# Interleaving expert steps with layer 3 in a four-layer attention chain, and moving one bias addition

## The chip, the cores and the metric

The kernel runs on one core of one Trainium2 chip. The time is the device time of one launch in microseconds (us), and the median of several runs is compared. The engines of the core are PE (TensorE, matrix multiplication, with PEld as its weight loads), DVE (VectorE), ACT (ScalarE), POOL (GpSimd) and SP (SyncE, which only issues transfers here). Each engine works through its own list of instructions in order.

## The reference

64 sequences of 128 tokens and 128 features pass through four layers in turn. Each sequence has a context of 77 rows. Cut to what matters here:

```
x = L0(ctx, x)        # layer norms, a small cross attention, a self attention
x = L1(x, ctx, ctx)   # linear attention with elu, residual, layer norm
# layer 2: self attention and cross attention of 16 heads of width 8, then 8 experts
x = x + mha(ln(x), ln(x));   x = x + mha(ln(x), ln(ctx))
h = ln(x);  top 2 of 8 experts by h @ router;  gates = softmax of the two
x = x + sum_k gate_k * (gelu(h @ w1[e_k] + b1[e_k]) @ w2[e_k] + b2[e_k])
# layer 3: causal self attention, cross attention, feed-forward, each with a layer norm after it
x = ln(x + sa(x) @ Wo + bo);  x = ln(x + ca(x, ctx) @ Wo + bo)
x = ln(x + relu(x @ W1 + b1) @ W2 + b2)
```

## The kernel before, in words

The 64 sequences are cut into 16 groups of 4 (`NB`); two groups make a set for the experts (`SG`), so there are 8 sets. The work of a group is written as Python generators. Each `yield` ends one step, and the order in which steps are emitted is written out by hand in the loop at lines 898 to 912. The framework derives the semaphores and may move instructions of neighbouring steps past each other on an engine, but the loop sets which steps stand side by side.

- `front` (L467) does layers 0 and 1 of a group in 7 steps.
- `middle` (L581) does layer 2 up to the router: two calls of `mha` of 8 steps each, then two steps for the router and the gates, and a last one that stores the group, so 19 in all. `firsts` (L874) runs `middle` of one group beside `front` of the next, so in steady state a group takes 19 rounds, and the first half of the kernel (layers 0 to 2) ends with round 299.
- `dispatch` (L666) works out for a set which token goes to which row of a DRAM buffer, in 2 steps, and scatters the tokens with 16 indirect transfers on POOL (L739), two to a step.
- `experts` (L755) works through the 23 tiles of 128 rows (`NT`) of a set, one tile to a step. It reads three tiles at once (L761), loads each tile's two expert matrices on SP (L774, L777, 256 KB each), and does a small bias product (L782), the first matrices (L787), one Gelu on ACT (L792) and the second matrices (L794). The result goes back to DRAM (L801). There are 184 such steps.
- `second_half` (L805) is layer 3 of a group. It gathers the experts' answers with 8 indirect transfers on POOL (L817), then calls `mha` twice and does the feed-forward, 18 steps. At most two groups are in it at once, in lanes 1 and 0; lane 0 is opened only when the first half is over. The dictionary `thirds` holds those that are open.

In every round of the loop, the first half gets one step (`ahead` is true while it lasts), then the dispatch, then perhaps the experts (L903), then each open layer-3 group.

`mha` (L336) has three parts. Its first step makes QT, KX and the values, and adds the residual and the output bias `bo` on POOL (L371) into `dst`; with `resid` None, as in layer 3's cross attention, it doesn't. Six steps then work on the four sequences in a pipeline: scores and softmax of sequence i (L387 to L399, in a PSUM tile `banks` of which there is one), the transposes of sequence i-1 (L409, L410), and the weighted sum and division of sequence i-2 (L417 to L432). The last step multiplies by the output matrix and adds to `dst` (L460). So the sum with `bo` is needed only at L460, seven steps after the first.

Of the kernel before, what the change touches and what calls it, by code (L numbers as in the profile page):

```python
# [11 lines left out]
ALU = mybir.AluOpType  # L12
# [9 lines left out]
NB = 4  # L22
# [30 lines left out]
def bc(ap, axis, n):  # L53

    ap = ap.unsqueeze(axis)
    shape = list(ap.shape)
    shape[axis] = n
    return ap.to_broadcast(shape)
# [11 lines left out]
def tile_xattn_chain(  # L70
# [21 lines left out]
    V, S, G, T = nc.vector, nc.scalar, nc.gpsimd, nc.tensor  # L92
# [13 lines left out]
    def bank():  # L106
        return ps1.tile([P, 512], F32, tag="bank", name="bank")
# [43 lines left out]
    row = {n: row_sb[:, i, :] for i, n in enumerate(ROWS)}  # L151
# [100 lines left out]
    n = x.shape[0] // NB  # L252
# [53 lines left out]
    def copy_t(src, p=P, **where):  # L306
        pool, tag = where.get("pool", work), where.get("tag", "tT")
        dst = pool.tile([P, NB * p], F32, tag=tag, name=tag, bufs=where.get("bufs"))
        S.copy(dst, transposed(src, p))
        return dst  # L310
# [25 lines left out]
    def mha(n, lane, qT, kT, nk, resid, dst, is_causal=False):  # L336
# [26 lines left out]
        for k, at in enumerate((0, 48)):  # L363
# [3 lines left out]
                bc(row[f"{n}_bv"][:nk], 1, NB).rearrange("k b (h i d) -> k b h i d", i=2, d=DH)[:, :, :, k],  # L367
                ALU.add,
            )
        if resid is not None:  # L370
            G.tensor_tensor(dst, resid, bc(row[f"{n}_bo"], 1, NB), ALU.add)  # L371
        yield
        O = work.tile([P, NB, P], F32, tag="O", name="O")

        def softmax(b):

            sc = banks()
            if is_causal:
                for g in range(4):
                    T.matmul(  # L380
                        sc[:, g, :], lhsT=ident16, rhs=causal16.rearrange("p j k -> p (j k)"),
                        start=True, stop=False,
                    )

            for g in range(4):
                part = slice(32 * g, 32 * g + 32)
                T.matmul(  # L387
                    sc[:, g, : NJ * nk].rearrange("q (j k) -> q j k", j=NJ),
                    lhsT=QT[part, b, :], rhs=KX[part, :, b, :nk],
                    start=not is_causal, stop=True,  # L390
                )
            halves = []
            for half in range(2):
                scores = sc[:, 2 * half : 2 * half + 2, : NJ * nk].rearrange("q i (j k) -> q i j k", j=NJ)
                m = small.tile([P, 2, NJ], F32, tag="m", name="m")
                recent["max"] = V.tensor_reduce(m, scores, AX.X, ALU.max)  # L396
                pr = attn.tile([P, 2, NJ, nk], F32, tag="pr", name="pr", bufs=4)
                V.tensor_tensor(pr, scores, bc(m, 3, nk), ALU.subtract)  # L398
                S.activation(pr, pr, AF.Exp, scale=DH**-0.5)  # L399
                halves.append(pr)  # L400
            return halves

        def turned(pr):

            pT = attn.tile([P, 2, NJ, P], F32, tag="pT", name="pT")
            for i in range(2):
                pt = bank()
                for j in range(NJ):
                    T.transpose(pt[:nk, j * P : (j + 1) * P], pr[:, i, j, :], ident)  # L409
                S.copy(pT[:nk, i].rearrange("k j q -> k (j q)"), pt[:nk])  # L410
            return pT

        def weighted(b, half, pT, po):

            for k in range(2):
                for g in range(4):
                    T.matmul(  # L417
                        po[32 * g : 32 * g + 32, half * P : half * P + P],
                        lhsT=vp[:nk, b, 4 * half + g, 32 * k : 32 * k + 32], rhs=pT[:nk, g // 2, g % 2 * 2 + k, :],
                        start=k == 0, stop=k == 1,  # L420
                    )

        def divided(b, po):
            oT = work.tile([P, 2, P], F32, tag="oT", name="oT")
            S.copy(oT.rearrange("p r q -> p (r q)"), po)
            on = bank()
            for r in range(2):
                T.transpose(on[:, r * P : (r + 1) * P], oT[:, r, :], ident)  # L428
            heads = on[:, 0 : 2 * P].rearrange("q (h c) -> q h c", c=16)
            rs = small.tile([P, NH], F32, tag="rs16", name="rs16")  # L430
            V.reciprocal(rs, heads[:, :, DH])  # L431
            V.tensor_tensor(  # L432
                O[:, b, :].rearrange("q (h d) -> q h d", d=DH), heads[:, :, 0:DH], bc(rs, 2, DH), ALU.mult
            )

        probs, turns = {}, {}
        for i in range(NB + 2):
            if i < NB:
                probs[i] = softmax(i)
            if i >= 2:  # L440
                po = pso.tile([P, 2 * P], F32, tag="po", name="po")
            if 0 <= i - 1 < NB:
                halves = probs.pop(i - 1)
                turns[i - 1, 0] = turned(halves[0])
            if i >= 2:
                weighted(i - 2, 0, turns.pop((i - 2, 0)), po)
            if 0 <= i - 1 < NB:
                turns[i - 1, 1] = turned(halves[1])
            if i >= 2:
                weighted(i - 2, 1, turns.pop((i - 2, 1)), po)  # L450
                divided(i - 2, po)
            yield
        OT = copy_t(O)
        ps = bank()
# [350 lines left out]
    def second_half(st, lane):  # L805
        t = st["t"]
        i = t // SG
        x4 = stream("x4")
        nc.sync.dma_start(out=x4.rearrange("q b d -> q (b d)"), in_=later_x[t])
        CT = work.tile([P, NB * SK], F32, tag="CTr", name="CTr", bufs=2)  # L810
        nc.sync.dma_start(out=CT, in_=later_c[t])
        se = st["set"]
        for b in range(NB):
            c = t % SG * NB + b
            for k in range(2):
                ans = work.tile([P, P], F32, tag="ans", name="ans", bufs=3)
                G.indirect_dma_start(  # L817
                    out=ans, out_offset=None, in_=answered[i],
                    in_offset=bass.IndirectOffsetOnAxis(ap=se["rows_i"][:, k, c : c + 1], axis=0),
                )  # L820
                V.scalar_tensor_tensor(
                    x4[:, b, :], ans, se["gates"][:, k, c : c + 1], x4[:, b, :], ALU.mult, ALU.add
                )
        yield


        xT = copy_t(x4)
        xs = stream("xs")
        yield from mha("3s", lane, xT, xT, P, x4, xs, is_causal=True)
        xh = normalize(xs)  # L830
        xT = affine_t(xh, "g1", "be1")
        xs = stream("xs")
        affine(xs, xh, "g1", "be1")
        yield from mha("3c", lane, xT, CT, SK, None, xs)
        xh = normalize(xs)
        xT = affine_t(xh, "g2", "be2")
        xs = stream("xs")
        affine(xs, xh, "g2", "be2")
        h1 = hidden(xT, ff_w1_sb, ff_b1_sb, AF.Relu)
        V.tensor_tensor(xs, xs, back(h1, ff_w2_sb), ALU.add)  # L840
        y = work.tile([P, NB, P], F32, tag="y", name="y", bufs=2)
        affine(y, normalize(xs), "g3", "be3", G)
        nc.sync.dma_start(out=out[t * NB : (t + 1) * NB].rearrange("b q d -> q b d"), in_=y)
        yield
# [29 lines left out]
    def firsts():  # L874


        yield from begun(0)
        yield from beside(beside(middle(states[0], 0), second_group()), begun_late(2, 19))
        done.extend(range(SG))
        for t in range(2, n):  # L880
            yield from beside(middle(states[t], 0), begun(t + 1) if t + 1 < n else iter(()))
            done.append(t)

    def sends():
        for i in range(n_sets):
            while (i + 1) * SG - 1 not in done:
                yield
            yield from dispatch(i)
            sent_sets.append(i)

    def seconds():
        for i in range(n_sets):
            while i not in sent_sets:
                yield
            yield from experts(i)
            answered_sets.append(i)

    first, send, second, thirds, t = firsts(), sends(), seconds(), {}, 0
    step = 0
    while t < n or thirds:  # L900
        ahead = next(first, "end") != "end"
        next(send, None)
        if step % 2 == 0 or not ahead:  # L903
            next(second, None)

        for lane in (1, 0):
            if lane not in thirds and t < n and t // SG in answered_sets and (lane or not ahead):
                thirds[lane] = second_half(states[t], lane)
                t += 1
            if lane in thirds and next(thirds[lane], "end") == "end":  # L910
                del thirds[lane]
        step += 1
# [74 lines left out]
```

## Time and profile before

| what | value |
|---|---|
| median of 3 runs | 3913.91 us (3906.8 to 3919.5) |
| the profiled execution's own time | 3934.11 us |
| its span, first to last instruction | 3932.3 us |
| PE busy | 3022.6 us, 77% |
| PE weight loads busy | 2063.3 us, 52% |
| DVE busy | 2153.0 us, 55% |
| ACT busy | 1977.9 us, 50% |
| POOL busy | 519.4 us, 13% |
| DMA moved | 180.81 MB, mean 46 GB/s |
| granted TensorE clock, mean | 0.832 of full |

"Busy" is time in which an engine executes; the shares are means over stages that differ. A "granted clock" below 1 means that matrix instructions ran slower for part of the time. Each view names an instruction by its line in the kernel and by the tiles that it writes and reads (out<-in). The windows view gives, for a stretch of the span, its length and then for each engine the busy time and, in brackets, the number of instructions, then the granted clock, the share of time the DMA engines were busy, and the GB/s.

### The profile page before, as it was taken

To read this page: it belongs to the slowest core of one execution; us is meant where nothing else is said; L and a number is where in the kernel's file an instruction comes from. 1 tells how busy PE (TensorE), PEld (TensorE's weight loads), DVE (VectorE), ACT (ScalarE), POOL (GpSimd) and SP (SyncE) were. 2 spreads that over 40 slices of the span, in tenths; PEclk is the share of its full clock that TensorE was granted. 3 is DMA by queue.
4 is the path that set the end of the run, shared out by engine and by line. 5 is a ranking of instruction groups with operands and counts; after the bars stand their busy time and mean duration, and the time that the engine had idled before them with its cause. 6 is when DMAs were issued, how large, how long until landed. Compare 5 with 4: busy or idle time off the path is not lost. (4 is left out here: it accounts for less than half of the span.)

```text
span 3932.3 us, 59072 instructions
## 1 busy us (share of the span) xinstructions
PE 3022.6 (77%) x22735; PEld 2063.3 (52%) x22797; DVE 2153.0 (55%) x5292; ACT 1977.9 (50%) x2994; POOL 519.4 (13%) x506
## 2 busy tenths in 40 slices
PE   3675677778778778787778877878878888878777
PEld 2454455545455555555455555656545555545544
DVE  5656454456465564555556645566445635445354
ACT  2443353545365554555454635656446556536344
POOL 1002101110211101101211012010210121020110
PEclk9776776878788787978788977989778989989988
DMA  5001111110111111111111011111111132222100
GB/s 178 2 10 35 45 37 55 48 43 30 47 37 43 46 37 33 43 38 52 39 32 53 28 55 39 41 37 36 37 46 40 43 104 65 63 83 64 62 8 6
DMA packets 168257, 180.81 MB, mean 46 GB/s; under 512 B 15708, under 2 KB 111784, under 8 KB 167848
## 3 DMA queue, kind: packets, MB, share of 16 engines
q1 hardware_dynamic: 157936, 157.03, 12.8%
q0 software_dynamic: 8192, 16.79, 1.4%
q8 instruction: 181, 2.97, 0.3%
q10 hardware_dynamic: 1848, 3.19, 0.2%
q14 instruction: 100, 0.82, 0.1%
HBM read 133.54 MB, written 43.42 MB: 45 GB/s over the span
## 5 line engine op out<-in xcount | busy, mean ns | idle before, releaser
L410 ACT COPY pT<-bank 77x512 f32<-77x512 f32 (+1 forms) x1024 | 565.8, 584 | 454.1 <-PE bank L409 410.5
L409 PE MATMUL bank<-ident,pr 128*128 128x128 f32 (+1 forms) x4096 | 661.5, 304 | 146.6 <-ACT pr L399 89.1
L396 DVE TENSOR_REDUCE m<-banks 128x8 f32<-128x1024 f32 (+1 forms) x512 | 514.6, 1005 | 432.3 <-PE banks L387 431.7
L409 PEld LDWEIGHTS bank<-ident,pr 128*128 128x128 f32 (+1 forms) x4096 | 506.7, 158 | 358.8 <-ACT pr L399 134.4
L398 DVE TENSOR_TENSOR pr<-banks,m 128x1024 f32<-128x1024 f32 (+1 forms) x512 | 513.7, 1003 | 26.7 <-PE bank L409 3.1
L399 ACT ACTIVATE pr<-pr 128x1024 f32<-128x1024 f32 (+1 forms) x512 | 451.5, 888 | 122.9 <-DVE pr L398 120.7
L387 PE MATMUL banks<-KX,QT 32*128 32x512 f32 (+1 forms) x2048 | 450.7, 659 | 51.7 <-DVE pr L398 39.6
L280 POOL TENSOR_TENSOR rs<-ve,mhalf 128x4 f32<-128x4 f32 (+1 forms) x160 | 164.4, 1027 | 2379.7 <-DVE ve L278 2379.3
L417 PE MATMUL po<-pT,vpad 77*32 77x128 f32 (+1 forms) x8192 | 435.3, 290 | 17.9 <-issue 8.2
L417 PEld LDWEIGHTS po<-pT,vpad 77*32 77x32 f32 (+1 forms) x8192 | 246.1, 112 | 145.8 <-issue 109.0
L794 PE MATMUL bank<-we,he 128*128 128x128 f32 x1472 | 246.1, 318 | 63.8 <-ACT he L792 60.7
L794 PEld LDWEIGHTS bank<-we,he 128*128 128x128 f32 x1472 | 209.9, 220 | 131.5 <-ACT he L792 103.7
L787 PEld LDWEIGHTS bank<-xT,we 128*128 128x128 f32 x1472 | 229.8, 227 | 60.7 <-ACT xT L769 32.6
L787 PE MATMUL bank<-xT,we 128*128 128x128 f32 x1472 | 241.9, 316 | 18.5 <-ACT xT L769 14.4
L296 PE MATMUL bank<-ident,xh 128*128 128x128 f32 (+1 forms) x448 | 97.0, 340 | 196.5 <-DVE xh L283 179.7
L792 ACT ACTIVATE he<-bank 128x512 f32<-128x512 f32 x184 | 109.9, 597 | 236.0 <-PE bank L787 227.8
L431 DVE RECIPROCAL rs<-bank 128x16 f32<-128x16 f32 x256 | 64.8, 253 | 290.3 <-PE bank L428 286.1
L387 PEld LDWEIGHTS banks<-KX,QT 32*128 32x128 f32 x2048 | 135.9, 213 | 144.2 <-issue 92.4
L739 POOL DMA_INDIRECT sent<-xm,rows_i x128 | 126.0, 984 | 525.7 <-DVE m L396 168.7
L296 PEld LDWEIGHTS bank<-ident,xh 128*128 128x128 f32 (+1 forms) x448 | 64.9, 167 | 223.5 <-issue 161.3
L792 ACT ACT_TABLE_LOAD x124 | 159.1, 1283 | 37.5 <-PE bank L787 35.5
L303 ACT ACTIVATE tT<-bank,col_sb 128x512 f32<-128x512 f32 x80 | 62.3, 778 | 182.6 <-PE bank L296 172.8
(242 smaller groups left out, 4055.3 us busy)
## 6 DMA issues: line engine op xcount, KB each, us to landing
we<-in_moe_w_dram SPq DMA_DIRECT2D x368, 256.0 KB
sent<-zero SPq DMA_DIRECT2D x56, 192.0 KB
xe<-sent SPq DMA_DIRECT2D x56, 192.0 KB
answered<-ye SPq DMA_DIRECT2D x56, 192.0 KB
X<-in_x_dram SPq DMA_DIRECT2D x16, 256.0 KB
later_x<-x3b SPq DMA_DIRECT2D x16, 256.0 KB
x<-later_x SPq DMA_DIRECT2D x16, 256.0 KB
out_dram<-y SPq DMA_DIRECT2D x16, 256.0 KB
```

The lines of the kernel that those rows point to most:

```text
L280: G.tensor_tensor(rs[:p], ve[:p], mhalf[:p], ALU.pow)
L296: T.transpose(ps[:, b * p : (b + 1) * p], src[:, b, :], ident[:p, :p])
L387: T.matmul(sc[:, g, : NJ * nk].rearrange("q (j k) -> q j k", j=NJ), lhsT=QT[part, b, :], rhs=KX[part, :, b, :nk], start=not is_causal, sto ...
L396: recent["max"] = V.tensor_reduce(m, scores, AX.X, ALU.max)
L398: V.tensor_tensor(pr, scores, bc(m, 3, nk), ALU.subtract)
L399: S.activation(pr, pr, AF.Exp, scale=DH**-0.5)
L409: T.transpose(pt[:nk, j * P : (j + 1) * P], pr[:, i, j, :], ident)
L410: S.copy(pT[:nk, i].rearrange("k j q -> k (j q)"), pt[:nk])
L417: T.matmul(po[32 * g : 32 * g + 32, half * P : half * P + P], lhsT=vp[:nk, b, 4 * half + g, 32 * k : 32 * k + 32], rhs=pT[:nk, g // 2, g % ...
L787: T.matmul(ps[:, c * P : (c + 1) * P], lhsT=we[:, 0, c, :], rhs=xT[:, a * P : (a + 1) * P], start=False, stop=c == NC - 1,)
L792: S.activation(he.rearrange("p c q -> p (c q)"), ps, AF.Gelu)
L794: T.matmul(eo[:, a * P : (a + 1) * P], lhsT=he[:, c, :], rhs=we[:, 1, c, :], start=c == 0, stop=c == NC - 1)
```

## The change

Two edits. In the loop, the experts were stepped in each even round, and in every round once the first half was over; now they are stepped in each even round, and in every round in which no layer-3 group is open at that point. In `mha`, the addition of residual and `bo` on POOL moves from the first step to the third of the six pipeline steps.

```diff
@@ mha, first step
-        if resid is not None:
-            G.tensor_tensor(dst, resid, bc(row[f"{n}_bo"], 1, NB), ALU.add)
         yield
         O = work.tile([P, NB, P], F32, tag="O", name="O")
@@ mha, for i in range(NB + 2)
                 weighted(i - 2, 1, turns.pop((i - 2, 1)), po)
                 divided(i - 2, po)
+            if i == 2 and resid is not None:
+                G.tensor_tensor(dst, resid, bc(row[f"{n}_bo"], 1, NB), ALU.add)
             yield
@@ the loop
-        if step % 2 == 0 or not ahead:
+
+        if step % 2 == 0 or not thirds:
             next(second, None)
```

## Prediction

> **What bounds the kernel now.** I read the engine table first, then the windows by stage and by group, the waits, and the timeline of the tail. The page says that no single engine is full:
>
> ```profile
> PE 3022.6 (77%) x22735; PEld 2063.3 (52%) x22797; DVE 2153.0 (55%) x5292; ACT 1977.9 (50%) x2994; POOL 519.4 (13%) x506
> ```
>
> So the time is made of chains that overlap imperfectly: a round costs what its streams (layers 0 and 1, layer 2, experts, layer 3) cannot hide behind each other. I cut the span by stage: after the first half (to 3163), the tail up to the end of set 6's experts (3474), the pair of groups 12 and 13 with set 7's experts (3723), the last pair alone.
>
> ```profile
> 810.00:3163.00 2353.00, 1883.30 (x14194) 1273.76 (x14233) 1347.75 (x3265) 1255.93 (x1890) 316.49 (x302) 0.83 0.13 40
> 3163.00:3474.00 311.00, 260.88 (x2114) 182.61 (x2121) 146.69 (x333) 169.84 (x256) 47.42 (x46) 0.94 0.26 80
> 3474.00:3723.00 249.00, 198.14 (x1563) 137.95 (x1571) 115.56 (x230) 129.17 (x194) 26.58 (x26) 0.89 0.22 69
> 3723.00:3933.00 210.00, 143.94 (x1157) 90.11 (x1164) 109.17 (x223) 86.81 (x143) 26.47 (x26) 0.84 0.03 9
> ```
>
> The reader is to see that the last stage, two layer-3 groups without experts, takes 210 us with PE busy only 144, so the stage before it carries set 7's 23 expert steps for only 39 us more. To price a layer-3 group beside the first half, I cut the first half by group (the Gelus at L792 and the exponentials at L399 appear in the order of the steps, so counting them dates each round):
>
> ```profile
> 341.00:493.00 152.00, 104.88 (x740) 76.31 (x741) 80.96 (x219) 63.94 (x99) 26.80 (x26) 0.71 0.15 47
> 493.00:659.00 166.00, 125.50 (x807) 86.69 (x806) 78.93 (x210) 77.88 (x112) 10.84 (x10) 0.74 0.14 46
> 838.00:1068.00 230.00, 182.03 (x1377) 121.93 (x1381) 132.05 (x322) 116.73 (x181) 21.36 (x20) 0.83 0.12 37
> ```
>
> Each is 19 rounds: with 5 expert steps and a dispatch; with 10 expert steps; with 10 expert steps and one whole layer-3 group. In the tail, experts alone come every 3.0 us:
>
> ```profile
> 3719.37 0.60 ACT L792 ACTIVATE he<-bank 128x512 f32<-128x512 f32 x1 [1.96 <-PE bank L787]
> 3722.38 0.60 ACT L792 ACTIVATE he<-bank 128x512 f32<-128x512 f32 x1 [2.42 <-PE bank L787]
> ```
>
> **What the Trainium skill says.** "Perfetto Trace Analysis", Identifying the Most-Contended Engine: matmul busy share is no measure of how near PE is to its limit, the weight-load share is a better one. The trace agrees that PE isn't full: weight loads are at 52%. "TensorE: Matmul & The Clock Gate", Part 1: PE falls to half clock after idle windows and comes back with sustained work. The granted clock was 0.71 to 0.74 in the two windows without layer 3 above and 0.83 in the one with it, which fits. "ScalarE: Activation LUTs", What ACT_TABLE_LOAD costs: 1283 ns plus a drain per change of function set; the L792 and L399 loads here are 1283 ns each, 124 and 108 of them. "Perfetto Trace Analysis", Tensor Engine Instruction: GpSimd's queue is strictly first in, first out, so an addition placed there delays what is behind it.
>
> **The change, part by part.** No instruction is added or removed; both edits move work. I ran the loop by hand with the yields of each generator.
>
> | | before | after |
> |---|---|---|
> | rounds | 375 | 374 |
> | layer-3 groups begun at rounds | 90, 109, 136 ... 293 | 67, 86, 116 ... 282 |
> | groups done inside the first half (to round 299) | 9 and 0.55 of the tenth | 11 |
> | expert steps up to round 299 | 128 | 147 |
> | expert steps beside first half and layer 3 | 84 | 94 |
> | beside first half only | 44 | 53 |
> | beside layer 3 only | 48 | 19 |
> | alone | 8 | 18 |
>
> *Layer 3 moved into the first half: +81 us.* A line through the twelve windows of one group each, from 493 us on, gives 165.6 us, plus 6 with a dispatch, plus 55.9 (standard error 7) for each whole layer-3 group beside it. 1.45 groups more cost 1.45 x 55.9 = 81. Bounds: 47 to 73 (the latter from a fit over all step types).
>
> *Nineteen more expert steps in the first half: +65 us.* The added price of a step there isn't seen alone. Its PE instructions take 0.38 + 1.05 + 1.16 + 0.2 = 2.8 us in the timeline. The window 341 to 493 had 4.5 fewer steps than the line's mean and took 152 against 165.6 + 6.2 = 171.8, 4.3 each; the front halves of two windows (0 and 4 steps, both with dispatch; 81.9 and 91.6 us) say 2.4. I take 3.4: 19 x 3.4 = 65. Bounds 1.4 (below) to 4.3; not below zero, since the PE work is real and PE is the busiest engine there.
>
> *The stretch from round 300 to the end of set 6: -168 us.* Before, it took 311 us: half of group 9, the pair 10 and 11, 33 expert steps. After, it holds group 11 alone with 9 expert steps, then 5 steps alone. A lone layer-3 group isn't in the profile. I build it from the last pair, whose exponentials date it: 34 us from the last Gelu to the first exponential, eight softmaxes of 7.7 (to 3820), 24 to the cross attention (3844), eight of 4.8 (to 3882), 50 to the end. Alone: 15 (8 gathers at 1.25 us instead of 16, and no wait for answers), 4 x 7.7 = 31, 20, 4 x 4.8 = 19, and 30 until the experts stand alone, so 115. Nine expert steps beside it at 1.4 make 128, and 5 x 3.0 = 15 follow: 143. 311 - 143 = 168. Upper bound of the lone group: only the second lane's softmaxes fall away from the pair, 210 - 31 - 19 = 160.
>
> *The pair 12 and 13: +7 us.* It hid 18 expert steps; the stage from 3474 to the 19th (3711) took 237, against about 200 for the last pair without its final store, so 2.1 each. With a step every second round only 10 lie beside it and 13 stand alone: 8 x (3.0 - 2.1) = 7. Bounds 0 to 16 (if the eight were hidden for 1.0). The last pair, 210 us, is unchanged.
>
> *The bias addition: -8 us.* 48 additions of 1.27 us, done by POOL, 61 us at most. DVE waited for POOL's `rs` (L280) for 163 us in 141 waits, 1.16 each, where `rs` itself takes 1.02; queueing is thus at most 20 us in all. The addition also stands among the 16 gathers that begin a pair, where it delays the next by one place. On the other side it can meet another stream's `rs` in its new round, at the same price. I take -8; bounds -20 to +10. The cover is the four steps left before L460.
>
> *The start of a layer-3 group: +5 us.* In rounds without layer 3 the experts' end is noticed one round later and not two, so the first gather follows the set's last expert step by one round in the first half. The tail shows 5 us from the last Gelu to the first gather (3722.4 to 3727.3). POOL waits in that time, and `rs` of the first half is queued behind it, with DVE's normalization waiting for that. Six times 0 to 5 us: 0 to 30. The reads at L761 now also follow the last scatter by one round in two sets, behind which SP's weight loads wait; I put that in the same sum.
>
> Sum: 81 + 65 - 168 + 7 - 8 + 5 = -18. The profiled execution's own time goes from 3934 to 3916. The median of the runs stands at 3913.91 / 3934.11 = 0.9949 of it: 3916 x 0.9949 = **3896 us**. A measurement here can tell about 0.3% (12 us) from no change.
>
> **The rivals.** *The experts are hidden in the first half.* For it: PE is busy only 75% in the windows without layer 3, at a clock of 0.74, and more matrix work can raise the clock. Against: the two estimates of 2.4 and 4.3. At 1.4 a step and a lone group of 115 us the sum is -18 - 38 - 13 = -69: 3845 us on the median's scale. *The lone group is a chain that nothing fills (slower).* Place: rounds 300 to 317, where lane 1 is empty, because set 6's answers are not ready. Price: each us of that group over 128 goes to the end. From 146 us on the gain is gone; at its bound of 160 the sum is +14 and 3928 us. For it: a single `banks` tile and one stream, so PE, DVE and ACT take turns, and PE cools. Against: half of group 9 with 10 expert steps and a dispatch took some 75 us in the trace. *The schedule only trades places.* The experts' and layer 3's work is the same, and 375 rounds become 374: within 12 us, 3914 us.
>
> **How the numbers follow.** The forecast 0.40, experts hidden 0.20, lone chain 0.27, traded places 0.13. Faster by over 0.3% is the first two, 0.60; same 0.13; slower 0.27. The forecast's own range is 3870 to 3905. The range of 8 in 10 reaches down to the hidden experts and up past the lone chain with expert steps at 4.3 (+17): 3842 to 3945. Both signs have weight; the likeliest case is faster.
>
> **What would show it.** In the changed kernel's trace: group 11 alone from about 3310 us on, for 115 to 130 us until the experts stand alone (more than 146 refutes the sum); 13 Gelus at 3.0 us before the last pair, where there were 5; the first half's end about 146 us later than 3163; the window of one group with a layer-3 group beside it still near 222 us; POOL's addition never followed by a longer wait of DVE for `rs` than 1.2 us in the mean. The prediction is wrong if a window without layer 3 and with an expert step in every round grows by more than 4.3 us a step, or if the first half stalls at the new gathers.

## The result, and the profile after

The changed kernel takes 3971.53 us (median of 4 runs, 3963.38 to 3980.23), the kernel before in the same runs 3912.03 us. The ratio is 1.0145, with a 95% interval of 1.0121 to 1.0170: slower by some 57 to 60 us, where 18 us less were forecast.

The profiled execution of the kernel after took 3963.38 us, with a span of 3961.6. That is 8 us under its median, while the profiled execution of before was 22 us above its own. So the two traces show a difference of 29 us, and not the whole 59. The rest can't be looked up in them, and the experiments below are therefore read by their medians and ratios first.

The engine line of the page after says, like that of before, that no engine is full:

```profile
PE 3052.0 (77%) x22797; PEld 2071.5 (52%) x22797; DVE 2147.2 (54%) x5292; ACT 1963.6 (50%) x2978; POOL 517.1 (13%) x506
```

PE's busy time seems to have grown by 29 us, but 62 of before's matmul records are missing (22735 of 22797; all are of the mask matmul, L380, which keeps PE busy for about 0.35 us), some 22 us. It is not a finding.

The windows by stage say more. I cut both traces at events that both have: the first expert Gelu, the first exponential of group 15's cross attention (the last group to pass through the first half), the last Gelu of set 6 and the last of set 7. First the kernel before:

```profile
433.00:3072.00 2639.00, 2083.18 (x15492) 1419.62 (x15526) 1479.08 (x3657) 1378.56 (x2069) 352.63 (x337) 0.82 0.13 42
3072.00:3474.00 402.00, 338.98 (x2701) 233.01 (x2713) 198.14 (x455) 222.61 (x334) 57.95 (x56) 0.93 0.24 73
3474.00:3723.00 249.00, 198.14 (x1563) 137.95 (x1571) 115.56 (x230) 129.17 (x194) 26.58 (x26) 0.89 0.22 69
3723.00:3933.00 210.00, 143.94 (x1157) 90.11 (x1164) 109.17 (x223) 86.81 (x143) 26.47 (x26) 0.84 0.03 9
```

And the kernel after:

```profile
431.00:3258.00 2827.00, 2265.11 (x16773) 1533.86 (x16777) 1562.97 (x3843) 1479.91 (x2215) 375.99 (x361) 0.83 0.14 44
3258.00:3500.00 242.00, 189.02 (x1469) 131.47 (x1467) 111.04 (x270) 116.43 (x181) 32.62 (x32) 0.85 0.20 61
3500.00:3749.00 249.00, 195.25 (x1571) 134.27 (x1571) 113.22 (x230) 119.76 (x186) 26.41 (x26) 0.91 0.22 67
3749.00:3962.00 213.00, 146.77 (x1164) 90.34 (x1164) 109.34 (x223) 87.22 (x144) 26.34 (x26) 0.83 0.03 9
```

The first numbers are the stretch and its length, then PE's busy time. The first half grew from 2639 to 2827, by 188 us. The three stages behind it fell from 861 to 704, by 157, nearly all of it in the first of them (402 to 242). The prediction had +146 and -161 there, with the cut at round 300, ten rounds behind the exponential used here. Round 300 has a Gelu in both kernels, at 3167.52 us in before and 3359.04 in after (the timeline of ACT, one line of each):

```profile
3167.52 0.60 ACT L792 ACTIVATE he<-bank 128x512 f32<-128x512 f32 x1 [0.34 <-PE bank L787]
3359.04 0.60 ACT L792 ACTIVATE he<-bank 128x512 f32<-128x512 f32 x1 [1.31 <-PE bank L787]
```

With that cut it is +193 up to there and -162 behind. So the loss is in the first half. PE's busy time rose by 182 us there (170 with the 34 missing records counted), and its idle time did not fall (556 to 562): the work that came in filled no gap.

The tail did what was forecast. Set 6's last five Gelus now stand alone, at the same pace as before (the timeline of ACT):

```profile
3488.56 0.60 ACT L792 ACTIVATE he<-bank 128x512 f32<-128x512 f32 x1 [1.31 <-PE bank L787]
3491.57 0.60 ACT L792 ACTIVATE he<-bank 128x512 f32<-128x512 f32 x1 [2.42 <-PE bank L787]
...
3499.74 0.60 ACT L792 ACTIVATE he<-bank 128x512 f32<-128x512 f32 x1 [2.42 <-PE bank L787]
```

The first half by group, again dated by counting Gelus and exponentials. These are the three windows of the kernel after that answer to 341 to 493, 493 to 659 and the one behind it. They hold 10, 13 and 5 expert steps, and none, 0.41 and one whole layer-3 group:

```profile
340.00:509.50 169.50, 122.11 (x833) 89.52 (x834) 82.53 (x222) 71.29 (x108) 26.77 (x26) 0.73 0.20 63
509.50:706.70 197.20, 147.45 (x1120) 100.71 (x1119) 110.77 (x266) 107.19 (x153) 27.58 (x26) 0.83 0.15 46
706.70:918.40 211.70, 176.38 (x1290) 118.11 (x1290) 128.17 (x310) 111.79 (x173) 33.81 (x33) 0.82 0.13 39
```

In the first of them only expert steps were added: five more for 17.5 us, 3.5 each. That is what the prediction had for one step (3.4).

A window with a layer-3 group beside the first half was to stay near 222 us. Two later ones, with a dispatch and most of a group (0.74 and 0.90), came out at 250 and 248. Of all these windows they lie furthest above the forecast; the one behind the second took 200 with a whole group. One window is therefore no measure of a group:

```profile
1583.80:1833.90 250.10, 209.15 (x1249) 138.09 (x1250) 114.26 (x284) 119.26 (x169) 38.28 (x38) 0.73 0.14 44
2054.40:2302.30 247.90, 195.05 (x1386) 129.42 (x1387) 136.44 (x341) 126.61 (x188) 47.10 (x45) 0.82 0.15 47
```

Of the waits, these rows of the kernel before (line, tile, what it waited for; us in total, times, longest us)

```profile
DVE xh L283 <- POOL rs L280: 146.8, 125, 7.0
DVE x L821 <- DMA ans<-answered,rows_i: 73.6, 66, 5.2
POOL ans L817 <- DMA answered<-ye: 43.5, 2, 31.6
```

became these after:

```profile
POOL ans L817 <- DMA answered<-ye: 158.8, 6, 53.9
DVE xh L283 <- POOL rs L280: 138.5, 124, 7.7
DVE x L821 <- DMA ans<-answered,rows_i: 97.2, 73, 7.1
```

POOL now waits six times, not twice, for the last answers of a set to land before it can gather them. It looks like the cause, and one of my theories was built on it. The experiments took it apart.

### The profile page after: what moved, and what is told of

It is laid out like the page before. It is cut to its first block, busy times and chain, and to the rows that moved or that the text cites. A ratio compares the mean times of both kernels' runs of the same rounds, so it can differ in the third digit from the quotient of the medians.

```text
span 3961.6 us, 59113 instructions
## 1 busy us (share of the span) xinstructions
PE 3052.0 (77%) x22797; PEld 2071.5 (52%) x22797; DVE 2147.2 (54%) x5292; ACT 1963.6 (50%) x2978; POOL 517.1 (13%) x506
## 5 line engine op out<-in xcount | busy, mean ns | idle before, releaser
L407 PE MATMUL bank<-ident,pr 128*128 128x128 f32 (+1 forms) x4096 | 670.2, 307 | 153.2 <-ACT pr L397 87.4
L394 DVE TENSOR_REDUCE m<-banks 128x8 f32<-128x616 f32 (+1 forms) x512 | 515.0, 1006 | 438.5 <-PE banks L385 428.4
L396 DVE TENSOR_TENSOR pr<-banks,m 128x616 f32<-128x616 f32 (+1 forms) x512 | 514.4, 1005 | 25.6 <-PE bank L407 2.8
L397 ACT ACTIVATE pr<-pr 128x616 f32<-128x616 f32 (+1 forms) x512 | 451.9, 888 | 149.2 <-DVE pr L396 137.3
L385 PE MATMUL banks<-KX,QT 32*128 32x512 f32 (+1 forms) x2048 | 477.9, 648 | 54.7 <-DVE pr L396 33.6
L415 PE MATMUL po<-pT,vpad 128*32 128x128 f32 (+1 forms) x8192 | 432.9, 289 | 15.2 <-ACT pT L408 13.5
L415 PEld LDWEIGHTS po<-pT,vpad 128*32 128x32 f32 (+1 forms) x8192 | 242.7, 112 | 147.0 <-issue 104.8
L385 PEld LDWEIGHTS banks<-KX,QT 32*128 32x128 f32 x2048 | 144.5, 210 | 152.9 <-issue 95.4
L817 POOL DMA_INDIRECT ans<-answered,rows_i x128 | 124.1, 970 | 265.6 <-DMA answered<-ye 158.8
```

Source lines behind the costliest of these rows:

```text
L385: T.matmul(sc[:, g, : NJ * nk].rearrange("q (j k) -> q j k", j=NJ), lhsT=QT[part, b, :], rhs=KX[part, :, b, :nk], start=not is_causal, sto ...
L415: T.matmul(po[32 * g : 32 * g + 32, half * P : half * P + P], lhsT=vp[:nk, b, 4 * half + g, 32 * k : 32 * k + 32], rhs=pT[:nk, g // 2, g % ...
```

## The experiments

Each ratio is to the kernel before, run on the same chip; the interval is 95%. Theory A began as: the loop edit costs it, because layer-3 groups begin in rounds that no expert step fills. From e5 on it was narrower: layer 3 now starts right behind the last expert step of its set, POOL waits there for the answers, and this costs more than 5 us a set. Its rivals were B, that the thinned expert steps in the tail lose time, and C, that the bias addition does.

| run | edit | median us | ratio |
|---|---|---|---|
| after | both edits | 3971.5 | 1.0145 (1.0121 to 1.0170) |
| e1 | loop edit alone | 3960.3 | 1.0114 (1.0090 to 1.0137) |
| e2 | bias edit alone | 3895.9 | 0.9939 (0.9916 to 0.9962) |
| e3 | after, tail dense again | 3947.4 | 1.0073 (1.0051 to 1.0095) |
| e5 | after, layer 3 one round later | 3917.5 | 1.0010 (0.9990 to 1.0030) |
| e6 | e5 and e3 | 3878.3 | 0.9900 (0.9873 to 0.9927) |
| e7 | after, layer 3 two rounds later | 3919.1 | 1.0022 (1.0008 to 1.0037) |
| e8 | bias edit, layer 3 one round later | 4034.4 | 1.0311 (1.0286 to 1.0335) |
| e9 | after, rows sent gathered | 3916.1 | 1.0012 (0.9991 to 1.0034) |
| e10 | before, rows sent gathered | 3860.0 | 0.9862 (0.9832 to 0.9892) |
| e11 | e6, bias addition back | 3884.3 | 0.9905 (0.9873 to 0.9938) |
| e12 | bias edit, layer 3 two rounds later | 3994.1 | 1.0199 (1.0168 to 1.0230) |
| e13 | before, expert steps moved alone | 3842.6 | 0.9834 (0.9808 to 0.9860) |
| e14 | e13, rows sent gathered | 3841.9 | 0.9839 (0.9814 to 0.9864) |
| e15 | before, layer 3 moved alone, rows sent gathered | 3921.5 | 1.0031 (1.0014 to 1.0047) |
| e16 | e1, rows sent gathered | 3906.2 | 0.9994 (0.9980 to 1.0009) |

**One edit at a time (e1, e2).**

```diff
@@ e1: the kernel before, with
-        if step % 2 == 0 or not ahead:
+        if step % 2 == 0 or not thirds:
@@ e2: the kernel before, with the addition moved from the first step to `if i == 2 and resid is not None`
```

> The loop edit alone; the bias addition stays in the first step of mha. Theory A (the loop edit costs it: layer-3 groups begin in rounds that have no expert step to fill them, and the first half grows by more than the tail gives back): slower than before by 45 to 70 us, like the whole change. Theory C (the bias addition, later in POOL's queue, does it): within 12 us of before.

> The bias edit alone; the loop as before. Theory A: within 12 us of before, with 8 us of gain as the prediction had it. Theory C: slower than before by 40 to 60 us.

The loop edit alone costs 1.14%, 45 us. The bias edit alone gains 0.61%, 24 us, more than forecast. They don't add up: 45 - 24 is 21, and the kernel with both is slower by 57. Why they meet so badly was not looked into. C is out as the cause of the whole, since the loop edit alone costs 45.

**The thinned tail (e3).**

```diff
-        if step % 2 == 0 or not thirds:
+        if step % 2 == 0 or not thirds or not ahead:
```

> The whole change, but experts stepped in every round again once the first half is over. The first half is that of the changed kernel. Theory A: still slower than before by 40 to 65 us, since the tail after the first half took as long as predicted. Theory B (thinning the experts in the tail costs it): back to within 15 us of before.

With a step in every round of the tail again, 0.72% (28 us) come back. B has a part in what is left on the table, but the kernel stays slower than before.

**Layer 3 starts later (e5, e6, e7).** A set counts as answered one round (e7: two rounds) after the loop has noticed it:

```diff
-    step = 0
+    step, noticed = 0, {}
...
+        for i in answered_sets:
+            noticed.setdefault(i, step)
         for lane in (1, 0):
-            if lane not in thirds and t < n and t // SG in answered_sets and (lane or not ahead):
+            if lane not in thirds and t < n and t // SG in answered_sets and step > noticed[t // SG] and (lane or not ahead):
```

> The whole change, but a layer-3 group begins one round later after its set's last expert step, as far behind it as before the change. Theory A in its narrow form (POOL waits in the first gather for the answers to land, and the normalizations of the first half wait behind it): gets back 20 to 40 us of the 60. If only the missing expert steps beside the start matter, or the experts' price: within 12 us of the changed kernel.

> The whole change, with a layer-3 group begun one round later after its set's last expert step, and experts in every round again after the first half. If the start (54 us) and the thinned tail (24 us) are separate costs, both are gone: about 3893 us, 0.5% faster than before, within 12 us of the bias edit alone (3896), which would say that dense experts in the first half bring nothing by themselves. If they overlap: 3905 to 3920.

> The whole change, with the start two rounds later. Theory A (from the last Gelu of a set to the first exponential of its layer-3 group is a chain of some 36 us that cannot be shortened, so each further round that stands inside it is nearly free): 10 to 40 us faster than with one round later, down to 3880 to 3905. If one round was all that the answers need to land (5 us): within 12 us of one round later (3917).

One round takes back 53 us of the 57, more than A's 20 to 40, and a second round gives nothing further. With the dense tail as well (e6) the kernel is faster than before by 1.0%. The stages of e5 and e6:

```profile
429.00:3208.00 2779.00, 2220.65 (x16668) 1507.22 (x16713) 1561.82 (x3838) 1468.41 (x2208) 377.12 (x362) 0.84 0.14 45
3208.00:3446.00 238.00, 187.72 (x1519) 131.45 (x1525) 108.89 (x275) 119.00 (x186) 31.52 (x31) 0.89 0.19 61
```

```profile
430.00:3203.00 2773.00, 2214.28 (x16670) 1499.99 (x16716) 1563.06 (x3838) 1469.32 (x2210) 376.16 (x362) 0.84 0.14 45
3203.00:3395.00 192.00, 159.63 (x1340) 111.16 (x1347) 97.24 (x235) 110.23 (x169) 28.23 (x28) 0.95 0.24 75
```

The gain of e5 is in the first half: 2827 to 2779.

**The same delay without the loop edit (e8, e12).** The kernel of e2 with e5's and e7's start.

> The bias edit alone (loop as before), with the start one round later than there. Theory A: there the chain already has one more round in it than in the changed kernel, so the gain is smaller, 0 to 25 us under 3896. If only the wait for the answers mattered: no gain, within 12 us of 3896.

> The bias edit alone, with the start two rounds later; one round later cost 138 us, which no theory here had. If layer 3 is worse the later it stands: 4040 us or more. If it is the place of layer 3's steps against the first half's that decides (each has its layer norm and its queries, keys and values in one step): different again, 3880 to 3960.

Every theory missed these. One round later costs 3.7% against e2 (146 us), two rounds 2.6%. The first half of e8 is 2735 us against e2's 2624 (windows cut at the same events; e2 first, then e8):

```profile
429.00:3053.00 2624.00, 2069.84 (x15496) 1408.90 (x15534) 1481.99 (x3659) 1379.19 (x2070) 350.61 (x336) 0.83 0.13 42
```

```profile
428.00:3163.00 2735.00, 2106.64 (x15479) 1427.57 (x15520) 1484.11 (x3656) 1386.24 (x2073) 350.05 (x337) 0.81 0.13 40
```

The same instructions, the same number of expert steps, every layer-3 group shifted by one round: +111 us. So "a later start is cheaper" is no rule. Where layer 3's steps stand against the first half's can weigh more than the 81 us that I charged for layer 3.

**No wait for the answers (e9, e10).** Layer 3 gathers the rows that were sent to the experts instead of their answers, so nothing in it waits for an expert step, while its groups still begin in the same rounds. The output is therefore another one.

```diff
-                    out=ans, out_offset=None, in_=answered[i],
+                    out=ans, out_offset=None, in_=sent[i],
```

> The whole change, but layer 3 gathers the rows that were sent to the experts in place of the experts' answers, so the result is another one; the gathers themselves stay, and nothing in layer 3 waits for the set's last expert step any more. Theory A: most of the 54 us comes back, 3905 to 3940, since the chain can begin before the last Gelu. If the cost is only that the eight gathers and their sums on DVE stand in a round without expert steps: within 15 us of the changed kernel's 3972.

> The kernel before, but layer 3 gathers the rows that were sent to the experts in place of their answers, so the result is another one: the control for the same edit on the changed kernel, which gained 56 us. Theory A (before the change, one more round stands between a set's last expert step and its first gather, and the chain of some 40 us is covered by four rounds): 0 to 20 us faster than before. If the edit gains by something else than the start (lighter gathers, an easier end): about 50 us faster here too.

In the changed kernel this gives 52 us, the same as e5. But e10, the control, gives 54 us in the kernel before as well. The wait is dear, and it was there already. With it gone from both, the changed kernel is still slower by 59 us (e9 against e10), as with it (57). So A falls as the cause of the loss. In its place I put a last theory, D: one of the two streams that the loop edit moves, the expert steps or layer 3, costs more at its new rounds than the sum charged.

**The bias addition in the repaired kernel (e11).** e6 with the addition back in the first step.

> The loop edit with both repairs (start one round later, experts in every round after the first half), and the bias addition back in the first step of mha: against the same with the moved bias (3878) it prices the bias edit a third time. If the bias edit is worth its 20 us wherever the loop is not stalled by starts: 3895 to 3905. If its worth depends on where the order of instructions happens to put it: within 12 us of 3878, or below.

0.9905 against 0.9900: no difference that these runs can tell.

**Each move alone (e13 to e16).** The rounds are written into the loop. Up to round 299, e13 has the expert steps in the rounds of the changed kernel (147 of them) and layer 3 in the rounds of the kernel before; e15 has it the other way round. Behind round 299 both step the experts in every round, as the kernel before does, and in e13 and e14 layer 3 begins there as soon as its answers are in and a lane is free. Only e16 has the thinned tail. e14, e15 and e16 gather the rows sent, so that layer 3 can be moved without the experts (their output is another one).

```diff
@@ e13, e14
+    dense = ((45, 65), (105, 115), (135, 135), (155, 159), (197, 199), (219, 219), (239, 241), (279, 281))
+    free = ((67, 81), (116, 119))
+    stepped = [
+        r for r in range(300)
+        if (r % 2 == 0 and not any(a <= r <= z for a, z in free)) or any(a <= r <= z and r % 2 for a, z in dense)
+    ]
+    starts = (90, 109, 136, 155, 182, 201, 228, 247, 274, 293) + (300,) * 6
...
-        if step % 2 == 0 or not ahead:
+        if step in stepped or not ahead:
...
-            if lane not in thirds and t < n and t // SG in answered_sets and (lane or not ahead):
+            if lane not in thirds and t < n and t // SG in answered_sets and step >= starts[t] and (lane or not ahead):
@@ e15
+    starts = (67, 86, 116, 135, 159, 178, 200, 219, 241, 260, 282, 300, 323, 323, 355, 355)
...
-            if lane not in thirds and t < n and t // SG in answered_sets and (lane or not ahead):
+            if lane not in thirds and t < n and step >= starts[t] and (lane or not ahead):
```

> The kernel before, with the expert steps in the rounds in which the changed kernel has them (147 up to round 299), while layer 3's groups keep the rounds in which the kernel before starts them. Nothing is left out. Read from the first half (first Gelu to the first exponential of group 15's cross attention; 2639 us in the kernel before). If the 3.4 us that the prediction gives an expert step in the first half is right: about +65 us there. If the price is the 4.75 us that a fit over the windows of all runs so far gives: about +90. If the experts cost nothing when layer 3 keeps its place: within 20. The time after the first half falls by about 40 in each case (19 steps of about 2 us less), so the whole comes to about +25, +50 or -40 us.

> The same move of the expert steps, and layer 3 gathers the rows sent to the experts in place of their answers, so that it waits for no expert step (its output is another one). Beside the kernel before with that gather (first half 2591 us): about +65 in the first half by the prediction's price of an expert step, +90 by the fitted one, the same as in the run with answers; clearly less than in that run if the moved steps cost mainly through the wait for answers.

> Layer 3 alone is moved: its groups start in the rounds of the changed kernel (67, 86, 116 and so on) while the experts keep every second round; possible because layer 3 gathers the rows sent and not the answers (its output is another one). Beside the kernel before with that gather (first half 2591 us): +81 in the first half by the prediction's price of 55.9 a group; +110 or more if the price of a group depends on where it stands against the first half and is higher at the changed kernel's rounds.

> The loop edit alone, with the gather of the rows sent (its output is another one): both moves together, without the bias edit. If the two moves add up, its first half is that of the kernel before with that gather plus what the two single moves added, within 20 us. If they cost extra together (dense expert steps, dispatch and a layer-3 group in the same rounds), it is over that sum by more than 20.

The first half and the rest, in the order e10 (neither moved), e14 (experts), e15 (layer 3), e16 (both), all with the rows sent gathered:

```profile
438.00:3029.00 2591.00, 2046.17 (x15492) 1395.81 (x15526) 1479.38 (x3658) 1376.70 (x2070) 347.82 (x334) 0.83 0.13 42
3029.00:3854.00 825.00, 668.12 (x5420) 457.31 (x5447) 422.00 (x908) 433.23 (x666) 111.20 (x108) 0.92 0.19 59
```

```profile
436.00:3064.00 2628.00, 2089.82 (x15864) 1435.56 (x15865) 1480.20 (x3664) 1410.89 (x2109) 347.15 (x334) 0.84 0.15 46
3064.00:3840.00 776.00, 631.64 (x5111) 424.23 (x5110) 415.17 (x902) 420.28 (x643) 111.07 (x108) 0.91 0.15 46
```

```profile
432.00:3206.00 2774.00, 2217.86 (x16430) 1491.28 (x16434) 1555.01 (x3836) 1454.51 (x2182) 374.04 (x359) 0.83 0.13 40
3206.00:3917.00 711.00, 566.13 (x4547) 391.99 (x4543) 337.14 (x729) 352.64 (x547) 85.11 (x83) 0.90 0.21 65
```

```profile
431.00:3214.00 2783.00, 2252.75 (x16769) 1523.41 (x16769) 1556.61 (x3842) 1479.50 (x2217) 374.05 (x359) 0.84 0.14 45
3214.00:3900.00 686.00, 533.57 (x4207) 360.85 (x4205) 331.95 (x723) 320.65 (x507) 85.12 (x83) 0.86 0.16 49
```

The nineteen expert steps alone: +37 us in the first half, -49 behind it. Layer 3 alone: +183 in the first half, -114 behind it. Both: +192 and -139. By the ratios of the whole (of 3912 us): the experts' move -9 us (the intervals of e10 and e14 overlap), layer 3's move +66, both +52. As the tails of these kernels differ in more than the moves, the whole is no test of whether the moves add up. The first half is one: there they come to 28 us less together than one by one. So their meeting costs nothing extra.

e13 is the same move of the experts with the real answers. Its two stretches, and its waits for answers:

```profile
429.00:3068.00 2639.00, 2102.32 (x15866) 1445.48 (x15867) 1481.13 (x3664) 1411.56 (x2108) 350.19 (x337) 0.83 0.15 46
3068.00:3844.00 776.00, 632.05 (x5109) 424.19 (x5108) 415.52 (x901) 419.88 (x643) 111.23 (x108) 0.90 0.15 46
```

```profile
POOL ans L817 <- DMA answered<-ye: 94.5, 3, 54.4
```

The first half is as long as in the kernel before, 2639 us, with nineteen more expert steps in it, and the rest is 85 us shorter. e13 and e14 take the same time (0.9834 and 0.9839): here the wait for the answers costs nothing. In the first half the last expert step of a set is 21 to 34 rounds old when layer 3 is let in. Most of e13's gain of 65 us is thus the 54 us that the kernel before loses to its wait. At 3842.6 us, e13 is the fastest kernel with the reference's computation: 1.7% under the kernel before, and 3.1% of it under the changed one. The row of POOL's wait is no price: before has 43.5 us in it and gains 54 when it is gone, e13 has 94.5 and gains nothing.

## Why the prediction was wrong

**Layer 3 moved into the first half: +81 us. This is the step that failed.** Alone it costs +183 there (e10 to e15), with no answers waited for and the experts at their old pace. I took 55.9 us a group from a line through the windows of the kernel before, and charged it for the 1.45 groups that were added (by the shares used here it is nearer 1.55, 5 us more), and nothing for the others, which only move. The price held for the rounds in which that kernel runs its groups: the same line through e10 gives 159.0 us a window, 7.9 more with a dispatch, and 58.6 a group. But the edit moved all of the groups to other rounds, and at the new ones they cost more in the mean. From round 54 to the start of group 15, e15's twelve windows (six with a dispatch) take 2635 us and hold 10.0 groups. If the rest of a window costs what it does in e10, that is (2635 - 12 x 159.0 - 6 x 7.9) / 10.0 = 68 us a group. The 1.51 groups added within these windows at 58.6 are 88 us; 9.4 more for each of ten are 94. Together they are the 182 us by which e15's windows exceed e10's. The 68 lies inside my bounds of 47 to 73; what failed is that it was owed for every group and not for the added ones alone. The sum of 182 is firmer than the price: a line through e15's own windows gives 66 us a group with a standard error of 18, and in e14, whose groups stand in the old rounds, it gives 73, with other expert steps from window to window.

That the same groups can cost more elsewhere is seen without a line from e2 to e8: the twelve windows of each hold 8.4 groups and as many expert steps, and one round's shift makes them 112 us longer, 13 us a group.

Why a group costs 68 at one place and 58 at another stays open. The wait for answers is not it (e15 has none), nor are dense expert steps (e15 has a step every second round). In e15 the added time is busy time of PE: +172 us in the first half (some 160 if e10's missing records are counted), and +11 of idle time. Its 938 more matmuls at e10's 132.1 ns of busy time each would be 124 us; that all of e15's take 135.0 ns adds 48. A single matmul took hardly longer (343 and 345 ns in the mean of the records), so fewer of them overlapped; whether that is cause or effect these runs don't tell. In e8 it is the other way round: +37 us of busy time and +74 of idle time against e2. So the two losses aren't of one kind. A count of the rounds in which the softmax steps of layers 2 and 3 meet explains nothing: up to the start of group 15 they meet in 32 rounds in before, in 24 after and in 36 in the faster e5.

**Nineteen more expert steps: +65 us.** Too much. It is 37 when they are moved alone and no answers are waited for, 9 beside the moved layer 3 (e15 to e16), and nothing on balance in e13, where the answers come early enough for the wait to go. The 3.4 us held in the one window where only steps were added (3.5), but not for the sum of the windows; what sets the price of a step was not found. For this term the rival "experts are hidden" (1.4 us a step, 27 in all) was nearer. The two errors, +102 and -28 to -56, partly cancel, so that the first half as a whole was off by 42 to 47 only (188, or 193 up to round 300, in place of 146).

**The stretch from round 300 to the end of set 6: -168 us.** It was -165 from the Gelu of round 300 on (306.1 us before, 140.7 after). The lone group with its nine steps took about 130 us (3359.04 to 3488.56), near the forecast's 128 and under the 146 from which the slower rival decides. Slower came true, but not by that rival's mechanism. **The pair 12 and 13: +7.** It was 0 (249 us and 249), and the last pair grew by 3.

**The bias addition: -8 us.** -24 alone, with an interval of -33 to -15 that goes past the lower bound of -20; +12 on top of the changed loop (1.0114 to 1.0145, intervals that overlap) and nothing to be told in the repaired kernel. The mechanism that I named, POOL's `rs`, shows little: DVE waited for it 138.5 us in 124 waits, 1.12 us each, against 146.8 in 125 before. So a gain of that size has another source, which was not looked for.

**The start of a layer-3 group: +5 us.** The term was a difference, and as such not far off: the wait for the answers is worth 54 us in before and 47 (e1 to e16) to 52 us after. What I missed is that before pays it already, some 9 us a set if six sets share it. It was not on my list, though POOL's row stood in its waits. e5's one round takes back just as much as gathering without a wait does (53 and 52). That it is the same time was not shown, as e5 also shifts layer 3 against the first half.

**The sum against one profiled execution.** The two traces differ by 29 us and the medians by 59. The sum missed the traces by 47 us (+29 against -18): with the cut at round 300, +50 in the first half with its bias and start terms, -1 behind it and -2 ahead of it. The other 30 us lie between single executions, and no view shows them.

## What to carry to other kernels

A price from windows of the running schedule holds for the places at which that schedule puts the work. An edit that shifts a whole stream against another one can reprice every unit of the stream, not only those that it adds: here 1.5 groups were costed, and ten were moved. When one edit moves two streams at once, pin each stream's rounds by hand and move them one at a time: it showed the expert steps of this edit, with layer 3 left where it was and the tail left dense, to be a gain (e13, -65 us) that the move of layer 3 buried. And try a theory about a wait on the kernel before too: it may pay for the same wait already.

## What was not expected of the hardware

The granted TensorE clock differs by stage far more than between kernels. It was 0.73 in the window of the kernel after without layer 3, 0.95 in e6's stretch up to the end of set 6, and between 0.81 and 0.84 over the first half of every kernel shown. Work that moves from the tail to the first half moves from a clock of 0.93 to one of 0.82. A shift of one round of 376 in the order of emission, with no instruction changed, moved the time by 146 us (e2 to e8), 3.7%.
